# Keys and values of the next images cut into pieces between attention blocks, and the projection in a pair of PSUM banks

## The chip, the cores and the metric

The kernel runs on one core of a Trainium2 chip (trn2). The metric is the device time of one execution in microseconds, the median of several runs. The engines are named as in the profile: PE (TensorE), PEld (its weight loads), DVE (VectorE), ACT (ScalarE), POOL (GpSimd), SP (SyncE).

## The reference

For 16 images of 64 channels and 128 x 128 points, the program applies two layers. The first adds a shift found from the median of each channel, then filters up, cuts at zero and filters down. The second is a spectral gate and an attention:

```python
xf = x + irfft2(spec * gate)                       # spectral gate
q = (x_flat @ q_w + q_b)                           # 16384 queries, 4 heads of 16
def kv_path(sr_w, sr_b, ln_g, ln_b, kv_w, kv_b, stride):
    xs = conv(xf, sr_w, stride) + sr_b             # 8x8 and 16x16, as long as the stride
    kv = layernorm(xs) @ kv_w + kv_b
    k, v = kv[..., :c], kv[..., c:]
    return k, depthwise3x3(v)
k, v = concat(kv_path(stride 8)), concat(kv_path(stride 16))   # 256 + 64 keys
out = softmax(q k^T / 4) v @ proj_w + proj_b
return out + x
```

All values are float32.

## The kernel before, in words

The function `phase1` runs the first layer and the spectral gate for all images and leaves its results in device memory. The function `phase2`, which the change touches, is the attention. It works through 512 blocks in a fixed loop: 16 images, 16 parts p of each, two halves f of each part, 512 queries in a block. An image thus has 32 blocks, and two images, whose keys and values are made together, have 64.

Within a block, a list called ORDER names what PE and DVE do, one after the other. S0 to S4 are the scores (tile `ss`) with their exponentials on ACT (tile `e`). M0 and M1, eight in a block, are products (tile `ma`) for the row maxima of the block two further on, each with a reduction on DVE (tile `nm`). V0, V1p and V2p are the products with the values (tile `av`). P is the queries of a later part (tile `qp`, method `queries`) where f is 0, and the projection of an earlier part (tile `pj`, method `project`, with its addition `ot` on DVE) where f is 1. After the second half of V2 the division runs in pieces between the maxima: `at`, `rd`, `at`, `on`, all on DVE. The maxima are turned (`nt`) and written into the query tile by four small transfers on SP's queue (`q<-nt`).

The helper `ordered` chains each of these instructions to the one before it on its engine, so PE and DVE keep the order of the program. Instructions outside the helper, and all of ACT's, POOL's and SP's, are placed by the framework's scheduler, by their place in the program and by when it takes their inputs and buffers to be free.

Scores, maxima and queries are written to `pair`, three rotating tiles of two PSUM banks each. The projection and all of `keys_values` use `misc`, a single bank. The values' sums use the eighth bank.

`keys_values(b, xp)` makes keys and values of two images: for each of the two strides a convolution of many small products summed in `misc` (`cp`), centering (`xs`, `center`, `xc`), variance and square root (`sq`, `var`, `sd`), reciprocal and scale (`sd`, `xc`, `yt`), the keys (`kp`, `kg`), the values (`vp`, `pad`), and nine taps of the depthwise filter on DVE (`vt`); at the end transposes (`vtp`) and copies (`vb`). It is called once before the loop, and then seven times, in the middle of the odd image of each two:

```python
if p == 0 and b % 2 == 0 and b + 2 < B:
    images = load_images(b + 2)
if p == NP // 2 and b % 2 == 1 and b + 1 < B:
    keys_values(b + 1, xps[b + 1])
```

Its input `xp`, two whole images, has one buffer, filled by 16 transfers on SP's queue that `load_images` yields one by one.

Of the kernel before, what the change touches and what calls it, by code (L numbers as in the profile page):

```python
# [8 lines left out]
F32 = mybir.dt.float32  # L9
# [3 lines left out]
ALU = mybir.AluOpType  # L13
# [4 lines left out]
B, C, H, W = 16, 64, 128, 128  # L18
# [4 lines left out]
NK1, NK2 = 256, 64  # L23
NK = NK1 + NK2
# [602 lines left out]
def phase2(ctx, tc, nc, cs, ident, vinit, w2, sr1, sr2, zd, xfd, out):  # L627
# [30 lines left out]
    def wt(name, rows=64):  # L658
        return w2s[0:rows, W2_AT[name]]
# [7 lines left out]
    def misc(name):  # L667
        return psm.tile([128, 512], F32, name=name, tag="m")

    def pair(name):  # L670
        return pss.tile([128, 2, 512], F32, name=name, tag="s")

    xps = {}
# [10 lines left out]

    c1, c2 = slice(0, NK1), slice(NK1, NK)

    def keys_values(b, xp):

        kgs = [kvp.tile([128, NK], F32, name=f"kg{b + i}", tag="kg", bufs=3) for i in range(2)]

        vts = [ks.tile([64, NK + NK2], F32, name=f"vt{b + i}", tag=f"vt{i}") for i in range(2)]
        for s, wgt, size, cols in (("1", s1, 16, c1), ("2", s2, 8, c2)):
            stride, m = H // size, size * size
            n = f"{b}_{s}"

            c_ps = misc(f"cp{n}")

            parts = 16 // stride
            src = xp.rearrange("p i (a d) (h f e) -> p (i a) d h f e", d=stride // 2, h=parts, f=stride)
            taps = [(d, f) for d in range(stride // 2) for f in range(stride)]  # L700
            for j in range(0, len(taps), 2):
                for y in range(2):
                    d, f = taps[j + y]
                    nc.tensor.matmul(  # L704
                        c_ps[64 * y : 64 * y + 64, 0 : 2 * m],
                        wgt[:, d, f, :],
                        src[:, :, d, :, f, :],
                        start=(j == 0),
                        stop=(j + 2 == len(taps)),
                    )  # L710
            xs = ks.tile([128, 2 * m], F32, name=f"xs{n}", tag="xs")
            nc.vector.tensor_scalar(
                xs.rearrange("p (a e h) -> p a h e", e=8, h=parts),
                c_ps[:, 0 : 2 * m].rearrange("p (a h e) -> p a h e", e=8, h=parts),
                wt("srb" + s, 128), None, ALU.add,
            )

            n_ps = misc(f"center{n}")
            nc.tensor.matmul(n_ps[0:64, 0 : 2 * m], cs("center"), xs, start=True, stop=True)
            xc = ks.tile([64, 2 * m], F32, name=f"xc{n}", tag="xc")  # L720
            nc.vector.tensor_copy(xc, n_ps[0:64, 0 : 2 * m])
            sq = ks.tile([64, 2 * m], F32, name=f"sq{n}", tag="sq")
            nc.vector.tensor_tensor(sq, xc, xc, ALU.mult)
            q_ps = misc(f"var{n}")
            nc.tensor.matmul(q_ps[0:64, 0 : 2 * m], cs("ones", 64)[:, 0:64], sq, start=True, stop=True)
            sd = ks.tile([64, 2 * m], F32, name=f"sd{n}", tag="sd")
            nc.scalar.activation(sd, q_ps[0:64, 0 : 2 * m], AF.Sqrt, scale=1.0 / C, bias=eps[0:64])
            nc.vector.reciprocal(sd, sd)  # L728
            nc.vector.tensor_tensor(xc, xc, sd, ALU.mult)
            yt = ks.tile([64, 2 * m], F32, name=f"yt{n}", tag="yt")  # L730
            nc.vector.tensor_scalar(yt, xc, wt("lng" + s), wt("lnb" + s), ALU.mult, ALU.add)


            k_ps = misc(f"kp{n}")
            nc.tensor.matmul(k_ps[:, 0 : 2 * m], wt("k" + s), yt, start=True, stop=True)
            for i in range(2):
                nc.vector.tensor_scalar(
                    kgs[i][:, cols], k_ps[:, m * i : m * i + m], wt("kb" + s, 128), D**-0.5, ALU.add, ALU.mult
                )
            v_ps = misc(f"vp{n}")  # L740
            nc.tensor.matmul(v_ps[0:64, 0 : 2 * m], wt("v" + s), yt, start=True, stop=True)
            pads = []
            for i in range(2):
                pad = ks.tile([64, size + 2, size + 2], F32, name=f"pad{n}{i}", tag=f"pad{size}", bufs=2)
                nc.gpsimd.memset(pad, 0.0)
                nc.vector.tensor_scalar(
                    pad[:, 1 : size + 1, 1 : size + 1],
                    v_ps[0:64, m * i : m * i + m].rearrange("p (a e) -> p a e", a=size),
                    wt("vb" + s),
                    None,  # L750
                    ALU.add,
                )
                pads.append(pad)
            for i in range(2):
                o = vts[i][:, cols].rearrange("p (a e) -> p a e", a=size)
                for tap in range(9):
                    src = pads[i][:, tap // 3 : tap // 3 + size, tap % 3 : tap % 3 + size]
                    w = dw[:, tap : tap + 1]
                    if tap == 0:
                        nc.vector.tensor_scalar(o, src, w, None, ALU.mult)  # L760
                    else:
                        nc.vector.scalar_tensor_tensor(o, src, w, o, ALU.mult, ALU.add)
        for i in range(2):
            vt = vts[i]
            nc.vector.tensor_copy(vt[:, NK : NK + NK2], vt[:, c2])
            t_ps = misc(f"vtp{b + i}")
            for j in range(3):
                nc.tensor.transpose(
                    t_ps[:, 64 * j : 64 * j + 64], vt[:, 128 * j : 128 * j + 128], ident[0:64, 0:64]
                )  # L770
            vb = vbs[(b + i) % 3]
            nc.scalar.copy(
                vb[:, 0:256].rearrange("p (a r) -> p a r", r=32)[:, :, 0:D],
                t_ps[:, 0:128].rearrange("p (a d) -> p a d", d=D),
            )
            for e in range(2):
                r = slice(64 * e, 64 * e + 64)
                nc.scalar.copy(
                    vb[r, 256:384].rearrange("p (a r) -> p a r", r=64)[:, :, 32 * e : 32 * e + D],
                    t_ps[r, 128:192].rearrange("p (a i d) -> p a i d", i=2, d=D)[:, :, e],  # L780
                )
            kv[b + i] = kgs[i], vb

    xas, zrs, qs, ops, nts, avs = {}, {}, {}, {}, {}, {}
    last = {}

    def ordered(op, *args, **kw):

        engine = op.__self__
        with tc.issue_after(last[engine]) if engine in last else nullcontext():  # L790
            last[engine] = op(*args, **kw).ins  # L791

    def product(*args, **kw):
        ordered(nc.tensor.matmul, *args, **kw)

    def load_part(tiles, tag, src, b, p):
        cut = slice(p * N, (p + 1) * N)
        t = io.tile([128, N], F32, name=f"{tag}{b}_{p}", tag=tag, bufs=2 if tag == "xa" else None)
# [122 lines left out]
            ops[self.at] = on  # L921

    def project(b, p):
        o_ps = misc(f"pj{b}_{p}")
        for f in range(2):
            product(o_ps[64 * f : 64 * f + 64, :], projw, ops.pop((b, p, f)), start=True, stop=True)
        cut = slice(p * N, (p + 1) * N)
        ot = io.tile([128, N], F32, name=f"ot{b}_{p}", tag="ot")
        ordered(nc.vector.scalar_tensor_tensor, ot, o_ps, projb, zrs.pop((b, p)), ALU.add, ALU.add)
        ov = out[b].rearrange("c (f h) w -> f c (h w)", f=2)  # L930
        for h in range(2):
            nc.gpsimd.dma_start(out=ov[h][:, cut], in_=ot[64 * h : 64 * h + 64, :])  # L932

    NP = HALF // N
# [2 lines left out]
    images = load_images(0)  # L937
    for _ in images:
        pass
    keys_values(0, xps[0])  # L940

    ORDER = "S0 M1 P M1 M0 V1p S1 M0 M0 V2p M1 S2 M1 V0 M0 S3 S4".split()

    def nothing(g):
        pass
# [11 lines left out]
    for i in range(len(blocks) + 1):  # L959
        b, p, f = blocks[i] if i < len(blocks) else (B, 0, 0)  # L960
        if f == 0 and i < len(blocks):
            if p == 0 and b % 2 == 0 and b + 2 < B:
                images = load_images(b + 2)
            if p == NP // 2 and b % 2 == 1 and b + 1 < B:
                keys_values(b + 1, xps[b + 1])
            if i + 6 < len(blocks):
                load_part(xas, "xa", xfd, *blocks[i + 6][:2])
                own_order(*blocks[i + 6][:2])
            load_part(zrs, "zr", zd, b, p)
        next(images, None)  # L970
        this = Block(b, p, f) if i < len(blocks) else None
        some = maxima(*blocks[i + 2]) if i + 2 < len(blocks) else nothing
        for what in ORDER:
            if what[0] == "V" and what[-1] == "p":
                if before is not None:
                    before.values(int(what[1]))
                    if what[1] == "2":
                        tail = before.divide()
                        next(tail)
            elif what[0] == "M":  # L980
                some(int(what[1]))
                next(tail, None)
# [79 lines left out]
```

## Time and profile before

| what | value |
|---|---|
| median of 3 runs | 11612.71 us (11609.7 to 11617.6) |
| the profiled execution | 11611.63 us |
| its span | 11609.8 us |
| PE busy | 10189.2 us (88%), mean granted clock 0.939 |
| DVE busy | 8352.8 us (72%) |
| ACT busy | 5524.1 us (48%) |
| POOL busy | 2502.4 us (22%) |
| first and last `cp` product | 5460.4 and 10719.7 us |
| first and last `pj` product | 5570.5 and 11602.7 us |

Times in the trace are counted from the start of the span. The attention takes its second half, from about 5400 us on. A row of the trace in order of time gives start, duration, engine, line, operation, the tiles written and read, their shape, the number of instructions merged, and in brackets how long the engine was idle before it and what ended that. A row of a stretch gives its bounds, its length, the busy time and count of PE, PEld, DVE, ACT and POOL (those that have any), the granted PE clock, the share of the transfer engines and GB/s. Where the helper `ordered` issued an instruction, the line shown is the helper's, 791, so instructions are told apart by their tiles.

### The profile page before, as it was taken

To read this page: it belongs to the slowest core of one execution; us is meant where nothing else is said; L and a number is where in the kernel's file an instruction comes from. 1 tells how busy PE (TensorE), PEld (TensorE's weight loads), DVE (VectorE), ACT (ScalarE), POOL (GpSimd) and SP (SyncE) were. 2 spreads that over 40 slices of the span, in tenths; PEclk is the share of its full clock that TensorE was granted. 3 is DMA by queue.
4 is the path that set the end of the run, shared out by engine and by line. 5 is a ranking of instruction groups with operands and counts; after the bars stand their busy time and mean duration, and the time that the engine had idled before them with its cause. 6 is when DMAs were issued, how large, how long until landed. Compare 5 with 4: busy or idle time off the path is not lost.

```text
span 11609.8 us, 175376 instructions
## 1 busy us (share of the span) xinstructions
PE 10189.2 (88%) x68096; PEld 4603.2 (40%) x68096; DVE 8352.8 (72%) x12025; ACT 5524.1 (48%) x7585; POOL 2502.4 (22%) x3370
## 2 busy tenths in 40 slices
PE   0668777787889999996999999999999999999999
PEld 0445444444445555553333333333333333333333
DVE  6978879779795555551777767767777677676777
ACT  0435444444445555552444545545445455454555
POOL 0224333343334444442000000000000000000000
PEclk9889888888889999998999999999999999999999
DMA  2121221221211111113212121121121211210111
GB/s 54 38 61 48 57 67 40 66 62 41 64 40 48 48 47 48 45 45 86 61 34 61 38 58 38 39 58 37 33 63 39 58 37 38 58 39 30 37 39 31
DMA packets 462689, 560.44 MB, mean 48 GB/s; under 512 B 80904, under 2 KB 344464, under 8 KB 459536
## 3 DMA queue, kind: packets, MB, share of 16 engines
q1 hardware_dynamic: 396304, 347.68, 13.2%
q0 software_dynamic: 65536, 201.39, 5.6%
q8 instruction: 538, 8.81, 0.3%
q14 instruction: 311, 2.55, 0.1%
HBM read 343.36 MB, written 201.33 MB: 47 GB/s over the span
## 4 chain that ended last, share of the span: by engine, by line
PE 48%; ACT 5%; DMA 1%; DVE 1%; SPq 1%; issue 1%; POOL 1%; ACTq 0%; POOLq 0%; DVEq 0%
PE av L791 13%; PE ma L791 13%; PE ss L791 12%; ACT e L881 4%; PE qp L791 3%; PE pj L791 2%; PE cp L704 2%; SPq L682 1%; PE bps L549 0%; DMA q<-nt 0%; DMA xp<-xfd 0%; DVE sd L728 0%; POOL sp L536 0%; PE rps L384 0%; PE yps L407 0%
## 5 line engine op out<-in xcount | busy, mean ns | idle before, releaser
L791 DVE TENSOR_REDUCE nm<-ma 128x2 f32<-128x640 f32 x4096 | 3240.9, 812 | 1272.1 <-PE ss L791 804.2
L881 ACT ACTIVATE e<-ss 128x1024 f32<-128x1024 f32 x2560 | 2620.7, 1024 | 2840.1 <-PE ss L791 2812.7
L791 PE MATMUL ss<-q,kg 32*128 32x512 f32 (+1 forms) x12288 | 2843.4, 635 | 32.5 <-DMA q<-nt 32.3
L791 PE MATMUL ma<-kg,q 32*128 32x320 f32 x16384 | 2763.6, 475 | 21.3 <-DVE nm L791 19.5
L791 PEld LDWEIGHTS ma<-kg,q 32*128 32x128 f32 x16384 | 1187.4, 185 | 1543.8 <-ACT e L881 803.9
L791 PE MATMUL av<-e,vb 128*32 128x512 f32 (+1 forms) x10240 | 1673.5, 610 | 0.0
L384 PE MATMUL rps<-up,w1s 128*128 128x262 f32 x4096 | 1116.3, 412 | 632.5 <-DVE up L374 367.6
L426 DVE SCALAR_TENSOR_TENSOR z<-y,w1s,z 128x512 f32<-128x512 f32 x1536 | 1314.1, 856 | 31.6 <-DVEq L324 3.1
L374 DVE SCALAR_TENSOR_TENSOR up<-pad,w1s,up 128x524 f32<-128x524 f32 x1280 | 976.9, 809 | 410.1 <-ACT up L372 330.7
L791 PEld LDWEIGHTS ss<-q,kg 32*128 32x128 f32 (+1 forms) x12288 | 728.4, 166 | 1293.6 <-DVE nt L791 397.6
L384 PEld LDWEIGHTS rps<-up,w1s 128*128 128x128 f32 x4096 | 767.7, 199 | 890.2 <-DVE up L374 307.2
L407 PE MATMUL yps<-r,w1s 128*64 128x262 f32 x4096 | 629.5, 422 | 364.1 <-ACT xf L576 337.9
L932 POOL DMA_DIRECT2D result<-ot x512 | 267.4, 527 | 2785.6 <-DVE ot L791 2751.7
L807 POOL COPY xo<-xa 128x512 f32<-128x512 f32 x256 | 272.1, 1064 | 2529.3 <-issue 2319.8
L386 ACT ACTIVATE r<-rps 128x524 f32<-128x524 f32 x1024 | 609.9, 611 | 337.4 <-PE rps L384 337.1
L183 DVE TENSOR_SCALAR_CACHE_REDUCE hit<-xm,t 128x4096 uint8<-128x4096 f32 x160 | 715.8, 4474 | 2.5
L357 POOL TENSOR_TENSOR pad<-pad,sb 128x512 f32<-128x512 f32 x256 | 302.7, 1183 | 1362.6 <-DMA pad<-x 1064.1
L549 PE MATMUL bps<-csb,sp 128*64 128x256 f32 x4096 | 565.1, 424 | 33.0 <-POOL sp L538 33.0
L424 DVE TENSOR_SCALAR z<-y,w1s 128x512 f32<-128x512 f32 x256 | 138.6, 541 | 584.9 <-ACT y L413 580.9
L407 PEld LDWEIGHTS yps<-r,w1s 128*64 128x64 f32 x4096 | 268.4, 144 | 726.7 <-ACT xf L576 377.6
L467 ACT ACTIVATE mag<-q 128x260 f32<-128x260 f32 x256 | 167.8, 655 | 790.9 <-POOL q L466 527.0
L355 POOL DMA_DIRECT2D pad<-x x256 | 200.6, 784 | 1584.6 <-DVE up L374 444.9
(151 smaller groups left out, 11481.5 us busy)
## 6 DMA issues: line engine op xcount, KB each, us to landing
xm<-x SPq DMA_DIRECT2D x32, 2048.0 KB
pad<-x POOLq DMA_DIRECT2D x256, 256.0 KB, 5.3
xfd<-xf POOLq DMA_DIRECT2D x256, 256.0 KB, 5.1
xp<-xfd SPq DMA_DIRECT2D x128, 512.0 KB
xa<-xfd SPq DMA_DIRECT2D x512, 128.0 KB
zr<-zd SPq DMA_DIRECT2D x512, 128.0 KB
result<-ot POOLq DMA_DIRECT2D x512, 128.0 KB, 2.9
zd<-z SPq DMA_DIRECT2D x512, 122.0 KB
```

Source lines behind the costliest of these rows:

```text
L183: nc.vector.tensor_scalar(hit, cut, thr, None, op, ALU.add, accum_out=cnt[:, j : j + 1])
L357: nc.gpsimd.tensor_tensor(xi, xi, shifts[b][:, c0 : c0 + G].unsqueeze(2).to_broadcast([128, G, W]), ALU.add).ins
L374: nc.vector.scalar_tensor_tensor(o, s, w, o, ALU.mult, ALU.add)
L384: nc.tensor.matmul(r_ps[:, i, 0:UP], ut[:, STAGES[k]], up[:, 2 * p + i, :], start=True, stop=True)
L386: nc.scalar.activation(t, r_ps[:, :, 0:UP], AF.Relu, scale=4.0)
L407: nc.tensor.matmul(y_ps[half, i, 0:UP], dr, r[k][:, i, :], start=True, stop=True)
L426: nc.vector.scalar_tensor_tensor(z, s, w, z, ALU.mult, ALU.add)
L549: nc.tensor.matmul(b_ps[64 * i : 64 * i + 64, 256 * q : 256 * q + 256], s[:, r, 2 * q + i, 0:64], cs("iv2" if r else "iv1"), start=(r == 0 ...
L791: last[engine] = op(*args, **kw).ins
L807: nc.gpsimd.tensor_copy(xo.rearrange("p (a e f) -> p a f e", e=8, f=16), xas[b, p].rearrange("p (a f e) -> p a f e", e=8, f=16),)
L881: nc.scalar.activation(e, s_ps, AF.Exp)
L932: nc.gpsimd.dma_start(out=ov[h][:, cut], in_=ot[64 * h : 64 * h + 64, :])
```

## The change

`keys_values` becomes a generator that yields after each of its pieces; counted in the code there are 64 of them (the change's short name says 62). Its PE and DVE instructions now go through `ordered` and so stand in the attention's own order on these two engines. It is started at block 13 of every 64, for the two images after the present two, and driven by two new entries of ORDER: K, at the end of a block, always runs the next piece; k, ahead of S3, runs one only when the piece is of the kind "rest". A piece of the kind "taps" is a sixteenth of a convolution. With one call, the convolutions take blocks 13 to 28 and 37 to 52, and the other pieces blocks 29 to 36 and 53 to 60. The key tiles are allocated when they are first written. The image loads are stepped twice a block. The projection takes a `pair` tile and uses one of its two banks, so that `misc` belongs to `keys_values` alone.

```diff
     def keys_values(b, xp):
-        kgs = [kvp.tile([128, NK], F32, name=f"kg{b + i}", tag="kg", bufs=3) for i in range(2)]
+        kgs = []
...
                     d, f = taps[j + y]
-                    nc.tensor.matmul(
+                    product(
                         c_ps[64 * y : 64 * y + 64, 0 : 2 * m],
...
+                if (j + 2) % (len(taps) // 16) == 0:
+                    yield "taps" if j + 2 < len(taps) else "rest"
             xs = ks.tile([128, 2 * m], F32, name=f"xs{n}", tag="xs")
-            nc.vector.tensor_scalar(
+            ordered(
+                nc.vector.tensor_scalar,
...
+            yield "rest"
             n_ps = misc(f"center{n}")
-            nc.tensor.matmul(n_ps[0:64, 0 : 2 * m], cs("center"), xs, start=True, stop=True)
+            product(n_ps[0:64, 0 : 2 * m], cs("center"), xs, start=True, stop=True)
+            yield "rest"
...
             nc.scalar.activation(sd, q_ps[0:64, 0 : 2 * m], AF.Sqrt, scale=1.0 / C, bias=eps[0:64])
-            nc.vector.reciprocal(sd, sd)
-            nc.vector.tensor_tensor(xc, xc, sd, ALU.mult)
+            yield "rest"
+            ordered(nc.vector.reciprocal, sd, sd)
+            ordered(nc.vector.tensor_tensor, xc, xc, sd, ALU.mult)
             yt = ks.tile([64, 2 * m], F32, name=f"yt{n}", tag="yt")
-            nc.vector.tensor_scalar(yt, xc, wt("lng" + s), wt("lnb" + s), ALU.mult, ALU.add)
+            ordered(nc.vector.tensor_scalar, yt, xc, wt("lng" + s), wt("lnb" + s), ALU.mult, ALU.add)
+            yield "rest"
...
                     if tap == 0:
-                        nc.vector.tensor_scalar(o, src, w, None, ALU.mult)
+                        ordered(nc.vector.tensor_scalar, o, src, w, None, ALU.mult)
                     else:
-                        nc.vector.scalar_tensor_tensor(o, src, w, o, ALU.mult, ALU.add)
+                        ordered(nc.vector.scalar_tensor_tensor, o, src, w, o, ALU.mult, ALU.add)
+                    if tap == 8 or size == 16 and tap % 3 == 2:
+                        yield "taps" if s == "1" and i == 1 and tap == 8 else "rest"
...
     def project(b, p):
-        o_ps = misc(f"pj{b}_{p}")
+        o_ps = pair(f"pj{b}_{p}")[:, 0]
...
-    keys_values(0, xps[0])
+    for _ in keys_values(0, xps[0]):
+        pass
+    keys, kind = iter(()), None
...
-    ORDER = "S0 M1 P M1 M0 V1p S1 M0 M0 V2p M1 S2 M1 V0 M0 S3 S4".split()
+    ORDER = "S0 M1 P M1 M0 V1p S1 M0 M0 V2p M1 S2 M1 V0 M0 k S3 S4 K".split()
...
-            if p == NP // 2 and b % 2 == 1 and b + 1 < B:
-                keys_values(b + 1, xps[b + 1])
...
-        next(images, None)
+        for _ in range(2):
+            next(images, None)
+        if i % 64 == 13 and b + 2 < B:
+            keys, kind = keys_values(b + 2, xps[b + 2]), "taps"
...
+            elif what == "K" or what == "k" and kind == "rest":
+                kind = next(keys, None)
```

More of the change, by code (lines that the diff above doesn't have):

```diff
@@ L685, in phase2, with ordered, product @@
     c1, c2 = slice(0, NK1), slice(NK1, NK)
+    last = {}
+    def ordered(op, *args, **kw):
+        engine = op.__self__
+        with tc.issue_after(last[engine]) if engine in last else nullcontext():
+            last[engine] = op(*args, **kw).ins
+    def product(*args, **kw):
+        ordered(nc.tensor.matmul, *args, **kw)
     def keys_values(b, xp):
-        kgs = [kvp.tile([128, NK], F32, name=f"kg{b + i}", tag="kg", bufs=3) for i in range(2)]
+        kgs = []
         vts = [ks.tile([64, NK + NK2], F32, name=f"vt{b + i}", tag=f"vt{i}") for i in range(2)]
@@ L716, in keys_values @@
             )
+            yield "rest"
             n_ps = misc(f"center{n}")
-            nc.tensor.matmul(n_ps[0:64, 0 : 2 * m], cs("center"), xs, start=True, stop=True)
+            product(n_ps[0:64, 0 : 2 * m], cs("center"), xs, start=True, stop=True)
+            yield "rest"
             xc = ks.tile([64, 2 * m], F32, name=f"xc{n}", tag="xc")
-            nc.vector.tensor_copy(xc, n_ps[0:64, 0 : 2 * m])
+            ordered(nc.vector.tensor_copy, xc, n_ps[0:64, 0 : 2 * m])
             sq = ks.tile([64, 2 * m], F32, name=f"sq{n}", tag="sq")
-            nc.vector.tensor_tensor(sq, xc, xc, ALU.mult)
+            ordered(nc.vector.tensor_tensor, sq, xc, xc, ALU.mult)
@@ L724, in keys_values @@
+            yield "rest"
             q_ps = misc(f"var{n}")
-            nc.tensor.matmul(q_ps[0:64, 0 : 2 * m], cs("ones", 64)[:, 0:64], sq, start=True, stop=True)
+            product(q_ps[0:64, 0 : 2 * m], cs("ones", 64)[:, 0:64], sq, start=True, stop=True)
+            yield "rest"
             sd = ks.tile([64, 2 * m], F32, name=f"sd{n}", tag="sd")
             nc.scalar.activation(sd, q_ps[0:64, 0 : 2 * m], AF.Sqrt, scale=1.0 / C, bias=eps[0:64])
-            nc.vector.reciprocal(sd, sd)
@@ L729, in keys_values @@
-            nc.vector.tensor_tensor(xc, xc, sd, ALU.mult)
+            yield "rest"
+            ordered(nc.vector.reciprocal, sd, sd)
+            ordered(nc.vector.tensor_tensor, xc, xc, sd, ALU.mult)
             yt = ks.tile([64, 2 * m], F32, name=f"yt{n}", tag="yt")
-            nc.vector.tensor_scalar(yt, xc, wt("lng" + s), wt("lnb" + s), ALU.mult, ALU.add)
+            ordered(nc.vector.tensor_scalar, yt, xc, wt("lng" + s), wt("lnb" + s), ALU.mult, ALU.add)
+            yield "rest"
             k_ps = misc(f"kp{n}")
-            nc.tensor.matmul(k_ps[:, 0 : 2 * m], wt("k" + s), yt, start=True, stop=True)
+            product(k_ps[:, 0 : 2 * m], wt("k" + s), yt, start=True, stop=True)
@@ L736, in keys_values @@
+            yield "rest"
             for i in range(2):
-                nc.vector.tensor_scalar(
+                if s == "1":
+                    kgs.append(kvp.tile([128, NK], F32, name=f"kg{b + i}", tag="kg", bufs=3))
+                ordered(
+                    nc.vector.tensor_scalar,
                     kgs[i][:, cols], k_ps[:, m * i : m * i + m], wt("kb" + s, 128), D**-0.5, ALU.add, ALU.mult
                 )
+            yield "rest"
             v_ps = misc(f"vp{n}")
-            nc.tensor.matmul(v_ps[0:64, 0 : 2 * m], wt("v" + s), yt, start=True, stop=True)
+            product(v_ps[0:64, 0 : 2 * m], wt("v" + s), yt, start=True, stop=True)
@@ L742, in keys_values @@
+            yield "rest"
             pads = []
@@ L745, in keys_values @@
                 nc.gpsimd.memset(pad, 0.0)
-                nc.vector.tensor_scalar(
+                ordered(
+                    nc.vector.tensor_scalar,
                     pad[:, 1 : size + 1, 1 : size + 1],
@@ L753, in keys_values @@
                 pads.append(pad)
+            yield "rest"
             for i in range(2):
@@ L759, in keys_values @@
                     if tap == 0:
-                        nc.vector.tensor_scalar(o, src, w, None, ALU.mult)
+                        ordered(nc.vector.tensor_scalar, o, src, w, None, ALU.mult)
                     else:
-                        nc.vector.scalar_tensor_tensor(o, src, w, o, ALU.mult, ALU.add)
+                        ordered(nc.vector.scalar_tensor_tensor, o, src, w, o, ALU.mult, ALU.add)
+                    if tap == 8 or size == 16 and tap % 3 == 2:
+                        yield "taps" if s == "1" and i == 1 and tap == 8 else "rest"
         for i in range(2):
             vt = vts[i]
-            nc.vector.tensor_copy(vt[:, NK : NK + NK2], vt[:, c2])
+            ordered(nc.vector.tensor_copy, vt[:, NK : NK + NK2], vt[:, c2])
+            yield "rest"
             t_ps = misc(f"vtp{b + i}")
             for j in range(3):
-                nc.tensor.transpose(
-                    t_ps[:, 64 * j : 64 * j + 64], vt[:, 128 * j : 128 * j + 128], ident[0:64, 0:64]
+                ordered(
+                    nc.tensor.transpose, t_ps[:, 64 * j : 64 * j + 64], vt[:, 128 * j : 128 * j + 128], ident[0:64, 0:64]
                 )
@@ L782, in keys_values @@
             kv[b + i] = kgs[i], vb
+            yield "rest"
     xas, zrs, qs, ops, nts, avs = {}, {}, {}, {}, {}, {}
[L785 to L794, printed above, removed]
     def load_part(tiles, tag, src, b, p):
```

## The prediction, made before the changed kernel was run

> **What bounds the kernel now.** I read the page first, then the stretches by block, then the order of time around one insertion of keys and values.
>
> ```profile
> PE 10189.2 (88%) x68096; PEld 4603.2 (40%) x68096; DVE 8352.8 (72%) x12025; ACT 5524.1 (48%) x7585; POOL 2502.4 (22%) x3370
> PE   0668777787889999996999999999999999999999
> PEclk9889888888889999998999999999999999999999
> ```
>
> From slice 20 on, the attention, PE is at 9: it sets the end. The next view gives the stretches with the instructions that touch `e` alone; the ACT count is five exponentials a block.
>
> ```profile
> 6185.00:6795.00 610.00, 179.73 (x1120) 28.69 (x1120) 286.06 (x280) 1.00 0.13 38
> 6304.80:7072.00 767.20, 208.44 (x1280) 33.22 (x1280) 327.81 (x322) 0.98 0.19 46
> 10905.50:11581.00 675.50, 199.00 (x1240) 31.77 (x1240) 317.03 (x311) 1.00 0.12 36
> ```
>
> Undisturbed, 56 blocks take 610 us, 10.89 each, and so do the last 62 (675.5 us). But 64 blocks with one call of `keys_values` take 767.2, not 697. The seven such stretches take 5368.2 us together, so the calls cost 5368.2 - 7 x 697.3 = **487 us, 69.6 each**. One of them, in order of time and by stretches:
>
> ```profile
> 6060.02 13.95 PE L704 MATMUL cp<-xp,s 128*64 128x512 f32 x64
> ...
> 6081.40 3.33 DVE L728 RECIPROCAL sd<-sd 64x512 f32<-64x512 f32 x1
> ...
> 6085.47 0.81 PE L791 MATMUL ma<-kg,q 32*128 32x320 f32 x4 [2.79 <-DVE nm L791]
> ```
>
> ```profile
> 6074.00:6086.00 12.00, 9.21 (x44) 2.54 (x44) 8.20 (x9) 6.56 (x7) 1.07 (x1) 1.00 0.07 22
> 6086.00:6097.20 11.20, 11.20 (x19) 2.36 (x16) 6.10 (x14) 0.00 (x0) 0.00 (x0) 0.51 0.00 0
> 6097.20:6112.60 15.40, 15.40 (x258) 15.21 (x256) 6.14 (x17) 2.31 (x2) 0.72 (x2) 0.91 0.01 2
> 6119.50:6137.50 18.00, 15.14 (x44) 4.44 (x44) 8.65 (x31) 3.94 (x9) 1.39 (x4) 0.53 0.59 107
> ```
>
> The convolutions stand in two blocks on PE, the reciprocal leaves PE idle for 2.79 us, and the granted clock falls to 0.51. Afterwards the next images' load holds PE once more:
>
> ```profile
> PE ss L791 <- DMA q<-nt: 4.9, 1, 4.9
> ```
>
> The undisturbed block, from ACT's, DVE's and PE's rows:
>
> ```profile
> 6411.82 3.10 ACT L881 ACTIVATE e<-ss 128x1024 f32<-128x1024 f32 x3 [1.29 <-PE ss L791]
> 6414.03 1.13 PE L791 MATMUL qp<-xo,w2s 64*128 64x512 f32 x4 [0.24 <-ACT e L881]
> 6422.86 3.10 ACT L881 ACTIVATE e<-ss 128x1024 f32<-128x1024 f32 x3 [1.29 <-PE ss L791]
> 6423.43 0.67 DVE L791 STREAM_TRANSPOSE on<-at 128x512 f32<-128x512 f32 x1
> 6424.76 1.08 PE L791 MATMUL pj<-on,w2s 128*64 128x512 f32 x4
> 6424.94 0.82 DVE L791 TENSOR_REDUCE nm<-ma 128x2 f32<-128x640 f32 x1 [0.84 <-PE ss L791]
> 6433.62 3.10 ACT L881 ACTIVATE e<-ss 128x1024 f32<-128x1024 f32 x3 [1.29 <-PE ss L791]
> ```
>
> The three ACT rows start 11.04 and 10.76 us apart: a block with queries (`qp`, in a PSUM pair) is 0.28 us longer than one with a projection (`pj`, in the single bank), and `qp` waits for an exponential.
>
> **What the Trainium skill says.** "TensorE: Matmul & The Clock Gate", Part 1, puts the fall to half clock after an idle window of about 3.4 us. This trace falls sooner, after the gap of 2.79 us: by my count over its clock record, each 3.41 us window less than half full of matmuls was followed by half clock, none over 0.6 full; so a gap of 1.5 us is enough. The same page, Part 3, has matmuls complete strictly in order; the trace agrees (nothing passes `cp`). "PSUM — Partial Sum Buffer", Specifications, gives eight banks; three pairs, `m` and `av` fill them, so `pj` takes one of the three pairs that scores and maxima rotate through.
>
> **Part 1, the projection.** The pair's third-last user is S4, as for `qp`. Of the ACT row at 6422.86, S4's exponential ends at 6424.94; `qp` started 0.14 us after its own. So `pj` moves from 6424.76 to 6425.08, its addition `ot` by as much, and the two maxima reductions behind it, whose pair the maxima after S1 wait for: 0.245 us by following the queue, 0.28 if the block takes exactly the query block's shape. 256 projections x 0.245 = **+63 us** (0 to 72; not below, since the bank given up costs nothing today).
>
> **Part 2, the steps.** The diff yields 64 times: 16 pieces of convolution at K in blocks 13 to 28, 16 other pieces two a block in 29 to 36, and again in 37 to 60. Per call:
>
> - Convolutions, 13.88 us and 15.38 x 0.91 granted clock = 14.0: **27.9**. PE is full, so nothing hides them.
> - Other matmuls: four of 512 columns at 1.07, four of 128 at 0.43, two transposes at 0.58: **7.2**.
> - PE pieces at k (`kp`, `vp`, twice) part M0 from S3, which overlap now: 4 x 0.7 = **2.8**.
> - PE pieces at K that wait for the DVE piece at k just before. DVE reaches k when `on` ends, 6424.10, which is 0.40 us after PE reaches K (6423.70). With 0.13 for the signal, PE waits 0.53 plus the DVE piece: `xs` 0.75, `xc`+`sq` 1.36, for the small path 0.35 and 0.56, the two `vt` copies 0.18 each. Sum 1.28 + 1.89 + 0.88 + 1.09 + 1.42 = **6.6**. Behind each stand the next block's S0 and maxima.
> - DVE pieces before the next block's first reduction. It has 0.84 us of room, and M0, which reuses its pair, some 0.2 more, so x us of DVE delay PE by x - 1.05: reciprocal, product, scale 4.53 -> 3.48; three blocks of two times three `vt` taps 2.35 -> 1.3 each; small reciprocal 0.46; all 18 small taps 3.6 -> 2.55. Sum **10.4**. `kg` and `pad`, 0.88, fit the room: 0.
> - The square root's table load, activation and reload on ACT (1.28 + 0.68 + 1.28): ACT is half idle, but they lie before S0's exponential: 0.2 to 0.8 each, taken **1.2** for two.
> - Clock: three of these gaps pass 1.5 us (1.9 at `var`, 2.6 at the reciprocal, where PE still has S0 to the second M1 to do, 1.8 at the small taps); two of three taken to fall inside a window, one or two windows of 3.41 us at half clock each, 2.5 us: **5** (0 to 18, if it lasts as in the burst).
> - Images: the two `next` calls do little, since today's loads already start at once after the last `cp` (6112.77), four blocks before their place in the code. SP issues 16 of them among the q rows; six loads cost about 5 us each (0 to 8): **4.3** a call.
>
> Sum 65.4, x 7 = **458 us** in place of 487. The gain of the spread is 29 us only.
>
> **Head.** The first call now keeps queries and maxima behind it on PE: +4 us (0 to 8). POOL's memsets and result DMAs keep their cover (POOL is 9% busy).
>
> **Total.** -29 + 63 + 4 = +38 us, on the profiled execution of 11611.63 (span 11609.8 and 1.8 around it), which lies 1.1 below the median 11612.71. I forecast **11650 us**, slower by 0.3%.
>
> **Rivals.** *Hidden waits (faster).* The 17 us of waits on DVE per call are my reading of an order that no row shows yet. If DVE runs ahead of PE by then, as its 77% in full blocks leave 2.4 us a block for, they shrink. From 5.4 us hidden a call the change is even, from 8.7 it is faster by 0.2%; with 11 hidden and the clock whole: 11650 - 7 x 16 = 11538. Against it: DVE's room lies elsewhere in the block, and the orders let nothing use it.
> *Projection free.* If the slot given to `pj` is one already released, 63 us go: 11587. For it: ACT is only 0.3 us late. Against it: `qp` waits in exactly this place.
> *Longer half clock (much slower).* If each trigger lasts the 11 to 18 us of the burst, 7 x 2 x 4.5 = 63 us more: 11713. For it: the rows above; against it: they lie among thin matmuls, here full blocks follow.
> *The change does not do what it says* in one point: the image loads, as above; if they now hurt nothing, -30 us.
>
> **Numbers.** A change within 0.2% (23 us) is about what measuring this kernel can't tell from none. Forecast and longer clock: 0.55 slower, of which 0.13 the latter. Projection free or waits partly hidden, within 0.2%: 0.19. Waits hidden, with or without the projection: 0.26. The range runs from 11545 (waits hidden) to 11735 (longer clock with its images at 8), the likeliest case alone from 11625 to 11690.
>
> **What would show it.** Right: projection blocks of 11.0 us outside the steps; convolution blocks 0.9 longer; blocks 30, 31 and 58 with PE gaps of 1.5 to 3 us and a clock of 0.5 after them; `cp` in pieces of about 1 us. Wrong: `pj` without a wait on `e`; reciprocal blocks no longer than their neighbours; stretches of 64 blocks under 750 us.

## The result, and the profile after

The changed kernel takes 11697.98 us (median of 4 runs, 11689.59 to 11705.5), the kernel before 11614.1 in the same comparison: ratio **1.0072**, 95% interval 1.0055 to 1.009, slower by 84 us. The forecast was 11650, slower by 38. The profiled execution took 11689.59 us with a span of 11687.7, 77.9 above the span of before.

First the page of the kernel after (span, the engines' row, PE and granted clock in 40 slices):

```profile
span 11687.7 us, 175329 instructions
PE 10172.8 (87%) x68096; PEld 4470.3 (38%) x68096; DVE 8391.4 (72%) x12025; ACT 5520.5 (47%) x7585; POOL 2506.6 (21%) x3370
PE   0668777787789999996999999999999999999999
PEclk9889888888999999997999999999999999999999
```

Busy times hardly moved (PE is even 16 us less busy), and PE is still at 9 from slice 20 on. The page doesn't show where 78 us went; the stretches do. As before the prediction, with the instructions that touch `e` alone, the ACT count being five exponentials a block:

```profile
7097.80:7873.70 775.90, 207.55 (x1280) 32.97 (x1280) 327.76 (x321) 0.99 0.18 45
10978.40:11659.30 680.90, 199.20 (x1244) 31.93 (x1248) 317.09 (x311) 1.00 0.12 35
```

The second row is undisturbed: 62 blocks take 680.9 us, 10.982 each, where before they took 675.5. The first is 64 blocks with one call of `keys_values` in steps: 775.9. Seven such groups take 5438.1 us in all, by the starts of the blocks' first exponentials; less 7 x 64 x 10.982 = 4919.9, the calls cost 518 us, **74 each**, where they cost 69.6. So the 78 us are made up thus: 518 - 487 = 31 for the calls, 43 for the projection (an undisturbed pair of blocks takes 21.96 us where it took 21.79; 0.17 x 256), and 3 at the head (the first block's exponential starts at 5540.1 instead of 5537.3).

What PE waits for in that group (releaser, us in all, times, longest):

```profile
PE ma L693 <- DVE nm L693: 9.0, 5, 3.4
PE ss L693 <- DMA q<-nt: 7.4, 1, 7.4
...
PE var L693 <- DVE sq L693: 2.5, 2, 1.7
PE center L693 <- DVE xs L693: 1.6, 2, 1.0
```

The waits are those of the forecast: maxima behind a long DVE piece, `var` and `center` behind the DVE piece of the half block before. The size of the DMA wait is not. In order of time, two places of this group:

```profile
7469.22 3.30 DVE L693 RECIPROCAL sd<-sd 64x512 f32<-64x512 f32 x1
...
7474.61 0.81 PE L693 MATMUL ma<-kg,q 32*128 32x320 f32 x4 [2.47 <-DVE nm L693]
...
7476.54 1.44 PE L693 MATMUL ma<-kg,q 32*128 32x320 f32 x4
...
7772.94 1.22 PE L693 MATMUL ss<-q,kg 32*128 32x512 f32 x2 [7.38 <-DMA q<-nt]
```

Behind the reciprocal PE idles 2.47 us, and a little later four maxima products take 1.44 us, where they took 0.81: half clock. Block 32 of the group thus lasts 17.45 us. In block 55 scores wait 7.38 us for the small transfer that writes the maxima into q. The stretches around the two, all instructions (PE, PEld, DVE, ACT, POOL busy, then granted clock, DMA share, GB/s), show the clock and, in the second, the cause:

```profile
7470.00:7480.00 10.00, 7.29 (x38) 2.57 (x36) 7.32 (x8) 3.44 (x5) 1.05 (x1) 0.83 0.10 29
7757.00:7776.00 19.00, 11.58 (x76) 3.72 (x76) 9.61 (x16) 5.98 (x6) 1.04 (x2) 0.83 1.12 202
```

The DMA engines are full, with the next images' 16 loads of 512 KB on SP's queue.

### The profile page after: what moved, and what is told of

Same layout as the page of the kernel before. It is cut to its first block, busy times and chain, and to the rows that moved or that the text cites. A ratio compares the mean times of both kernels' runs of the same rounds, so it can differ in the third digit from the quotient of the medians.

```text
span 11687.7 us, 175329 instructions
## 1 busy us (share of the span) xinstructions
PE 10172.8 (87%) x68096; PEld 4470.3 (38%) x68096; DVE 8391.4 (72%) x12025; ACT 5520.5 (47%) x7585; POOL 2506.6 (21%) x3370
## 4 chain that ended last, share of the span: by engine, by line
PE 45%; ACT 6%; DVE 3%; DMA 1%; POOL 1%; issue 1%; SPq 1%; ACTq 0%; POOLq 0%; DVEq 0%
PE ma L693 13%; PE av L693 13%; PE ss L693 12%; ACT e L904 6%; PE cp L693 2%; PE qp L693 1%; PE pj L693 1%; DVE vt L693 1%; DVE nm L693 1%; SPq L682 0%; DVE on L693 0%; PE bps L549 0%; POOL sp L536 0%; DMA q<-nt 0%; PE rps L384 0%
## 5 line engine op out<-in xcount | busy, mean ns | idle before, releaser
L693 PEld LDWEIGHTS ma<-kg,q 32*128 32x128 f32 x16384 | 1156.4, 186 | 1688.4 <-ACT e L904 876.1
```

## Experiments

The two theories after the result: **(T)** the projection's turn in the pairs costs 43 us, and each step's cost comes from its place: a long DVE piece ahead of the maxima, a product one half block behind its DVE piece, the image load at one go. **(R)**, the rival: the steps stall PE whatever their shape, so what is removed in one place comes back in another. Ratios are against the kernel before, run beside on the same chip. For the kernel after the ratio is 1.0072. "By ratio" means that a difference between two kernels is taken from their ratios.

### The projection's pair alone, on the kernel before

```
-        o_ps = misc(f"pj{b}_{p}")
+        o_ps = pair(f"pj{b}_{p}")[:, 0]
```

> The kernel before with one edit: the projection's product goes into one bank of a pair of the three rotating PSUM pairs instead of the single bank; keys and values stay undivided in their old place. Theory (the pair is what the projection costs: its turn in the ring puts ScalarE's exp or VectorE's maximum one place back): a pair of blocks takes 21.96 us instead of 21.79, +0.165 us x 256 projections = +42 us, so about 11656 us against 11614. Rival (the projection is as good as free in the ring, and all of the 84 us comes from the 62 steps): 11614 us within 10 us.

Measured: 11666.06 us, ratio 1.0042 (1.0028 to 1.0056): +47 us on this chip's 11619.04. The span grew by 54.4. 60 undisturbed blocks take 10.984 us each, as in the kernel after (10.985), against 10.900. The projection's products and weight loads in one plain stretch of 120 us, of the kernel before and then of this one (busy, mean ns, then idle before it and its releaser):

```profile
L791 PE MATMUL pj<-on,w2s 128*64 128x512 f32 x24 | 6.5, 618 | 0.0
L791 PEld LDWEIGHTS pj<-on,w2s 128*64 128x64 f32 x24 | 1.2, 134 | 3.1 <-issue 3.1
```

```profile
L791 PE MATMUL pj<-on,w2s 128*64 128x512 f32 x20 | 5.4, 618 | 0.7
L791 PEld LDWEIGHTS pj<-on,w2s 128*64 128x64 f32 x20 | 1.0, 134 | 3.7 <-ACT e L881 3.7
```

Before, the load of `projw` waits for nothing but its turn; in the pair it waits for an exponential, as the forecast read from the block with queries. PE, which did not idle ahead of the products before, now idles 0.7 us ahead of five projections, 0.14 each. So the pair is shown to cost 0.17 us a projection (twice 10.984 - 10.900), 43 to 47 us in all, half of what the change lost.

### Image loads in their place

Each load is ordered behind the latest `q<-nt` transfer on SP's queue, so that it can't start before its place in the program.

```
-                    nc.sync.dma_start(out=xp[64 * y : 64 * y + 64, i, r : r + 16], in_=v[y][:, r : r + 16])
+                    with tc.issue_after(last[nc.sync]) if nc.sync in last else nullcontext():
+                        nc.sync.dma_start(out=xp[64 * y : 64 * y + 64, i, r : r + 16], in_=v[y][:, r : r + 16])
...
-                nc.sync.dma_start(out=rows[s], in_=nt[32 * s : 32 * s + 16, :])
+                last[nc.sync] = nc.sync.dma_start(out=rows[s], in_=nt[32 * s : 32 * s + 16, :]).ins
```

> The kernel after with one edit: each of the 16 image loads of a call is put behind the latest small DMA that writes the maxima into q on SyncE's queue, so that they start where the program has them (two a block over the first eight blocks) and no longer all at once as soon as the old images are free. Theory (the load at once delays the small DMAs that block 55 and 56 of a group wait for, 8.6 us in each of six groups): 11698 - 52 = 11646 us, block 55 at about 10 us instead of 16 to 18, and no wait of 7 us for the q<-nt transfer. Rival (the images' 4 MB cost the same wherever they lie, or the small taps' stall just moves there): 11698 us within 15.

(The loads are 16 x 512 KB, 8 MB and not 4, by the page's list of DMA issues.) Measured: 11650.54 us, ratio 1.0029 (1.0017 to 1.0042), so 50 us less than the kernel after, by ratio; the profiled run was the fastest of six, 11621.4. Block 55 takes 9.75 us instead of 18.14. The waits for a window that holds the same group no longer have a DMA in them, while the maxima wait for DVE as they did:

```profile
PE ma L694 <- DVE nm L694: 9.0, 5, 3.4
```

The theory's size held. Blocks 0 to 7, in which the loads now go out two at a time, take 11.04 and 10.93 us in turn, as in the kernel after. So the load of 8 MB costs nothing there, and cost 8.7 us where the queue let all 16 run ahead among the small transfers.

### The two images' taps in turn

```
-            for i in range(2):
+            for at in range(18):
+                tap, i = at // 2, at % 2
...
-                for tap in range(9):
...
+                if (at + 1) % (3 if size == 16 else 9) == 0:
```

> The kernel after with one edit: VectorE's nine taps of the two images are issued in turn (image 0 tap 0, image 1 tap 0, image 0 tap 1 ...) with the same 6 + 2 pieces, instead of all of one image and then all of the other. Theory (each tap of the same image waits for the one before it to be through, so it takes 0.50 us at 64x256 and 0.30 us at 64x64, against 0.40 and 0.20 in turn): the two small pieces go from 2.47 to about 1.7 us and the six large ones from 1.5 to 1.2; blocks 34 to 37 and 59, 60 are 4 to 6 us shorter in all, x 7 = 28 to 42 us: about 11663 us. Rival (the pieces are long enough to stall the maxima either way and the half clock after the stall sets the price): 11698 us within 12.

Measured: 11647.23 us, ratio 1.0024 (1.0015 to 1.0033), 56 us less than the kernel after, by ratio; the span fell by 42.3. The kernel after and this one in order of time on DVE, large taps and small:

```profile
7537.36 3.00 DVE L693 SCALAR_TENSOR_TENSOR vt<-pad,w2s,vt 64x256 f32<-64x256 f32 x6
7810.01 2.47 DVE L693 SCALAR_TENSOR_TENSOR vt<-pad,w2s,vt 64x64 f32<-64x64 f32 x8
```

```profile
7527.82 2.42 DVE L693 SCALAR_TENSOR_TENSOR vt<-pad,w2s,vt 64x256 f32<-64x256 f32 x6
7800.09 3.21 DVE L693 SCALAR_TENSOR_TENSOR vt<-pad,w2s,vt 64x64 f32<-64x64 f32 x16
```

Six large taps in a chain take 3.00 us, in turn 2.42: 0.50 and 0.40 each. Small ones take 0.31 and 0.20. Blocks 36 and 59 fall from 14.62 and 17.95 us to 11.97 and 15.36. The forecast had priced the taps from the kernel before, where they stood in turn; the change had taken that apart as well.

### One step a block

```
-    ORDER = "S0 M1 P M1 M0 V1p S1 M0 M0 V2p M1 S2 M1 V0 M0 k S3 S4 K".split()
+    ORDER = "S0 M1 P M1 M0 V1p S1 M0 M0 V2p M1 S2 M1 V0 M0 S3 S4 K".split()
...
-                if (j + 2) % (len(taps) // 16) == 0:
+                if (j + 2) % (2 if s == "1" else 16) == 0:
...
-        if i % 64 == 13 and b + 2 < B:
+        if i % 64 == 8 and b + 2 < B:
```

The two copies of the small values move into the steps of the small taps.

> The kernel after, with its steps put only in the last place of a block (the extra place ahead of scores 3 is gone), from block 8 of the 64 on, in 54 pieces: the second scale's taps in 8 pieces instead of 16, the copies of the small values in the piece of the small taps. Same work, one piece a block. Theory (a product and the VectorE piece that it waits for now lie a block apart, and no block gets two VectorE pieces): the waits of center and var (1.28 + 1.89 us a call as predicted, 2.8 measured), the splits of the two half places (2.8) and part of the double pieces' stalls and of the half clock after them are gone, 8 to 14 us a call x 7: about 11620 us. Rival (the stalls are set by the size of a piece and by the image load, not by two pieces falling in one block, and longer tap pieces cost as much): 11685 us or above.

Measured: 11624.98 us, ratio 1.0006 (0.9998 to 1.0015): 77 us less than the kernel after, by ratio. In the waits of one group `var` and `center` are gone; the reciprocal and the image load are not:

```profile
PE ss L693 <- DMA q<-nt: 7.8, 2, 7.3
...
PE ma L693 <- DVE nm L693: 4.2, 3, 2.5
```

The kernel is a compound of edits (one place, fewer and larger pieces of the second convolution, the copies moved, an earlier start), so the 77 us are not shared out among them. Of the group's waits, the 4.1 us of `var` and `center` and 4.8 of the 9.0 at the maxima behind DVE are gone, while the waits of maxima for exponentials rose from 3.6 to 7.4 us.

### The reciprocal in four

```
-            ordered(nc.vector.reciprocal, sd, sd)
+            for at in range(0, 2 * m, 128):
+                ordered(nc.vector.reciprocal, sd[:, at : at + 128], sd[:, at : at + 128])
+                if s == "1":
+                    yield "rest"
```

> The kernel after with one edit: the first scale's reciprocal of 512 columns, one VectorE instruction of 3.48 us, becomes four of 128 columns in four steps (two of them ahead of scores 3, two at a block's end). Theory (the maxima behind the long reciprocal wait 2.5 us, and the clock is halved after that gap: block 32 takes 17.45 us): with pieces of 0.87 us neither happens, block 32 falls to about 12, less some 1 us of later double pieces: 5 us a call x 7 = 35 us, ratio 1.004 where the kernel after has 1.0072. Rival (the clock is halved once after these stalls whatever starts it, so the next double piece brings it on): ratio 1.006 or above.

(The whole reciprocal takes 3.30 us and each part 0.90; the 3.48 of the expectation is the forecast's delay, not a duration.) Measured: 11665.73 us, ratio 1.0044 (1.003 to 1.0058), as the theory has it; but the span fell by 18.1 only. Block 32 falls from 17.45 us to 11.04. But block 38, which now holds the taps that block 36 had (14.62 us), takes 16.24. PE waits 1.35 us for the maxima there, as it did in block 36; the stretches show that in this group the clock is now halved for longer:

```profile
7540.00:7546.00 6.00, 4.41 (x24) 1.26 (x20) 5.17 (x8) 2.70 (x4) 1.56 (x2) 0.82 0.16 45
7546.00:7552.00 6.00, 6.00 (x36) 2.19 (x28) 2.39 (x5) 1.02 (x1) 0.00 (x0) 0.61 0.01 3
```

At a mean of 0.82 and 0.61 the two make (0.18 + 0.39) x 6 x 2 = 6.8 us of half clock, where the 30 us around block 36 of the kernel after had 0.94, or 3.6 us. Over all seven calls the clock records put it elsewhere. Around these taps half clock is 34 us in both kernels. After block 32 there were 30.7 us of it, and none is left; but after block 30, with `var`, it rose from 13.7 to 47.8 us, and the sum over the calls is 170.7 us in both kernels. Here the rival is partly right: of 6.4 us gained in block 32 of this group, nearly all was given back (775.4 us for the 64 blocks against 775.9), in other groups less. Runs and trace differ by 15 us on the size; it stays at 18 to 33.

### The projection at the end of the order

```
-    ORDER = "S0 M1 P M1 M0 V1p S1 M0 M0 V2p M1 S2 M1 V0 M0 k S3 S4 K".split()
+    ORDER = "S0 M1 P M1 M0 V1p S1 M0 M0 V2p M1 S2 M1 V0 M0 k S3 S4 R K".split()
...
-            elif what == "P" and f == 1 and i > 2:
+            elif what == "R" and f == 1 and i > 2:
```

> The kernel after with one edit: in blocks of f = 1 the projection stands behind scores 4, at the end of the block's order, instead of ahead of the second maximum. Theory (the pair costs 0.165 us a projection because its turn in the ring, drained by VectorE, falls among the maxima, where the next user of that pair waits for it; between scores 4 and the next block's scores 0 VectorE has no maximum due): 0.165 us x 256 = 42 us come back, up to 60 with those of the blocks with steps: about 11650 us where the kernel after has 11700 on this scale (1.0072 of before). Rival (any seventeenth turn in the ring costs the same wherever it stands, or at the end it delays the next block's first exponential): no change, ratio 1.007, or above.

Measured: 11810.6 us, ratio 1.0172 (1.0158 to 1.0186), 116 us slower than the kernel after. The theory fell. PE from scores 4 to the values, of the kernel after and then of this one:

```profile
11559.78 0.54 PE L693 MATMUL ma<-kg,q 32*128 32x320 f32 x2
...
11560.82 1.08 PE L693 MATMUL pj<-on,w2s 128*64 128x512 f32 x4
11561.86 0.82 PE L693 MATMUL ma<-kg,q 32*128 32x320 f32 x8
```

```profile
11513.31 0.54 PE L693 MATMUL ma<-kg,q 32*128 32x320 f32 x2
...
11513.68 1.47 PE L693 MATMUL ma<-kg,q 32*128 32x320 f32 x6
11515.38 0.81 PE L693 MATMUL ma<-kg,q 32*128 32x320 f32 x4 [0.23 <-ACT e L904]
```

From the first row to the end of the maxima is 2.90 us with the projection in between (11559.78 to 11562.68) and 2.88 without (11513.31 to 11516.19). So nearly equal a length, with a wait on `e` at the end of the second, says that the stretch is held by the pairs coming free and not by PE; the projection's 1.08 us stood in a hole. Moved away it leaves the hole, and adds its time where there is none: blocks of f = 1 take 11.77 us instead of 10.92.

### Fine steps: the edits that paid, together

The last place of a block only, from block 9, in 53 steps; loads behind the small transfers; the reciprocal in four; taps in turn, the large ones beside the second scale's convolution:

```
+                    if s == "2":
+                        for _ in range(2 if j + 2 < 112 else 3):
+                            next(large)
```

> The kernel after with four edits that earlier runs priced one by one, and one new: steps in the last place of a block only; the image loads behind the small DMAs; the two images' taps in turn, the large ones two at a time beside the second scale's convolution; 53 steps from block 9; new: the first scale's reciprocal in four steps of 128 columns (0.87 us each instead of 3.48 at once). Theory (losses add up: the one-place kernel's groups of 64 blocks take 767 us, of which block 30, with the reciprocal, 6.8, the image load in blocks 50 and 51 some 12.5, the small taps 3.3 over a plain block): 745 us a group, where 32 x 0.95 us of convolution is nearly all that is left over 703 plain: 11480 us, ratio 0.988. Rival (a stall taken away shows the next one, the clock drops once a group whatever is done, or loads at two a block delay blocks 0 to 8 instead): ratio 0.995 or above.

Measured: **11448.78 us, ratio 0.9859 (0.9844 to 0.9874)**: 163 us faster than the kernel before and, by ratio, some 250 faster than the kernel after. Of all that were run it is the fastest. One group of 64 blocks takes 743.2 us, and in it PE waits for no DVE piece and no DMA any more:

```profile
7029.20:7772.40 743.20, 205.85 (x1280) 32.89 (x1280) 327.38 (x320) 1.00 0.19 47
```

```profile
PE ma L694 <- ACT e L920: 4.6, 17, 1.7
```

The longest wait left, 1.7 us, is the exponential behind the square root's table loads. By count over the clock record of the trace, the granted clock fell 4 times in the seven calls, against 31 in the kernel after. Image loads, taps, reciprocal and places gave 50 + 56 + 33 + 77 = 216 us one by one, by ratio; together they give 247. The gains add up. The 30 us more are not clear of the noise, since all four gains are counted from the kernel after, whose own ratio is known to 20 us either way. Nor does the clock explain them: half clock in the calls fell from 171 us to 14, by 157, and one by one the four edits took away 82, 48, 0 and 17 of it, 147 in all. What the new place of the large taps gave was not tried by itself.

### Fine steps with the projection at the end

> The kernel of the fine steps (in place of a block's end only, loads behind the small DMAs, taps in turn, reciprocal in four) with the projection behind scores 4 as well. Theory: the two gains add up, 42 us less than the fine steps alone: about 11440 us, ratio 0.985. Rival (at the end of a block the projection and a step stand in the same place, so what the projection gives in plain blocks is lost in the 53 blocks with a step): within 10 us of the fine steps alone.

Measured: 11634.76 us, ratio 1.0019 (1.0011 to 1.0027), 186 us slower than the fine steps alone. Neither theory nor rival: 186 / 256 = 0.73 us a projection, which is what an undisturbed pair of blocks shows in both kernels with the projection at the end (22.69 us against 21.96: 0.85 more at f = 1, 0.12 less at f = 0). With coarse steps 0.73 x 256 = 186 us had shrunk to 116. The blocks show where: over the seven groups, the projection at the end adds 0.84 us to a plain block of f = 1 and 0.69 to one with a convolution step, with coarse steps as with fine ones, but with coarse steps blocks 29 to 36, where PE waits for DVE, come out 2.9 us a call shorter in all (blocks 32 and 36 by 2.3 and 2.9). Half clock in the calls is 140 us there, against 171 in the kernel after. That the projection fills a part of those waits is likely, and not tried by itself.

## Why the prediction was right, and by what errors

The direction was right, and the time lies in the range, though above the likeliest case's own 11690. A part of that was luck: the steps were forecast to gain 29 us and lost 31, so that their sign was wrong. Slower was forecast only because the projection's loss, itself too large by nearly half, outweighed that gain. The loss was 84 us instead of 38, 46 more, and two terms missed in opposite ways:

| term | predicted | measured |
|---|---|---|
| projection, 256 | +63 | +43 (+47 alone) |
| calls, seven, against 487 | -29 | +31 |
| head | +4 | +3 |

The head's 3 us are within what it varies by. The first block starts at 5541.4 us in the kernel before with the projection's pair alone, whose first call is undivided, and at 5538.3 with the image loads in their place, which has the new head.

**The projection**: mechanism right, size 0.17 us instead of 0.245. The sum had followed S4's exponential to the addition `ot` and the maxima; the wait was there. That a part of it fell in time that the maxima would have waited anyway, the hole that the moved projection laid bare, is the likely reason for the rest, and not tried by itself.

**The calls**, one of them (the group of the rows above), split as in the forecast: each block is set against a plain one of its kind, and blocks 55 and 56, for the images, against the last call, which has no load behind it (9.76 and 12.24 us instead of 18.14 and 12.57). Block 37 holds a convolution step as well as a delay; 0.96 us of it count as the step. From blocks 32, 59 and 60 a key product (1.1 us) and two sets of transposes (0.6 each, by block 60) count with the rest:

| per call, us | predicted | measured |
|---|---|---|
| convolution steps, blocks 13 to 28 and 37 to 52 | 27.9 | 30.6 |
| DVE delays with the clock, blocks 32, 35 to 37, 59 | 15.4 | 18.5 |
| images | 4.3 | 8.7 |
| the rest: products, k split, waits at K, table loads | 17.8 | 15.3 |
| sum | 65.4 | 73.1 |

Three terms were too small, images by 4.4 us, DVE delays with the clock by 3.1 and convolution steps by 2.7; the rest was too large by 2.5.

- **DVE delays and clock**: the small taps, priced at 3.6 us for all 18 from the kernel before, take 5.4, for in a chain each waits for the last; and the clock's 5 us counted two drops a call where there are 4.4. This is the step that failed most, by experiment: its 3.1 us in the table are what is left beside other delays that were over-priced. The taps in turn took back 42 us of span, 6 a call; the fine steps, which leave 4 drops in all, took back the clock with the gaps.
- **Images**: the forecast saw that the loads start early, and gave them today's cost. In the kernel before one wait of 4.9 us showed; here 7.38 and half clock after it, six times a run. That is 6 x 8.7 = 52 us a run for the forecast 7 x 4.3 = 30, and the experiment that holds the loads in place took back 50.
- **The rest** was over-priced: `center` and `var` waited 1.01 and 1.67 us where 1.28 and 1.89 stood, and the small path's sums of 0.88 and 1.09 came to 0.61 and 0.87.
- Convolution steps are 0.96 us each where 0.87 was taken for them.

Of the rivals, *hidden waits* is out: the waits are in the rows. *Projection free* fell by the experiment on the kernel before. *Longer half clock*, 11713, came nearest in time but not by its cause: the drops are short, mostly one or two windows of 3.41 us and never more than three (by the clock record 171 us of half clock in the calls, against 259 before), only more of them: 31 against 20. That the image loads "do nothing" is right in the sense that the two `next` calls set nothing, and wrong on their cost.

"TensorE: Matmul & The Clock Gate", Part 1, of the Trainium skill puts the fall to half clock after about 3.4 us of idleness. The kernel after shows it after gaps of 2.47, as the kernel before did after 2.79; the forecast's own limit, none over 0.6 full, was a little low: of the 31 drops of the kernel after, five followed windows 0.6 to 0.7 full and two windows 0.71 full, and none a fuller one.

## What to carry to other kernels

When one long piece of work is cut into steps between other work, price each step by what stands behind it on its engine: a step of 0.9 us fitted where one of 2.4 or 3.3 us cost its excess and then half clock as well, and a product that stood a whole block behind the vector step it needs no longer waited for it. Transfers that a program spreads over its loop are only spread if something orders them; otherwise they can run ahead, as here, and delay the small ones. Before work is moved to another place in the critical engine's order, ask whether it stands in a hole there: the projection cost 0.17 us where it stood and 0.73 more at the end of the block, where DVE had no maximum due.

## What was not expected of the hardware

- VectorE's `scalar_tensor_tensor` on its own last output took about 0.10 us more than with another one in between, at both sizes here: 0.50 against 0.40 us at 64 x 256, 0.31 against 0.20 at 64 x 64.
- While 8 MB went in at about 190 GB/s on the same queue, a set of four transfers of 2 KB held the scores up for 7.38 us; with two loads of 512 KB a block, no wait on them shows.
